# A transformer layer with routed experts: where the posts' weights are rounded, and the order of the work behind the attention

## The chip, the cores and the metric

The kernel runs on one core of a Trainium2 chip. The metric is the device time of one execution in microseconds. The core's engines run their own instruction streams and meet at semaphores: TensorE (PE in the profile; its weight loads are PEld), VectorE (DVE), ScalarE (ACT), GpSimd (POOL, "Pool" in the code) and SyncE (SP), which issues the DMA transfers.

## The reference

`x` is (4, 2048, 256) in float32: four sequences, 16 heads of 16 channels, 8 experts.

```python
# first: x = x + attn(layernorm(x)); attn adds its own input once more
qkv = einsum('bld,ed->ble', x, w_qkv) + b_qkv            # q, k, v: 16 heads of 16
attn = softmax(einsum('blhc,bmhc->bhlm', q, k) / 16)
heads = einsum('bhlm,bmhc->blhc', attn, v).reshape(b, l, d)
return einsum('bld,ed->ble', heads, w_o) + b_o + x
# then: x = x + ffn(layernorm(x)), with xf the 8192 tokens
scores = softmax(xf @ w_gate.T)                          # over the 8 experts
s = (scores + expert_bias).reshape(N, 4, 2)              # 4 groups of 2 experts
# keep the 2 groups with the largest sums, in them the 2 best experts: topk_idx
weights = take_along_axis(scores, topk_idx, 1)
counts = bincount(topk_idx.reshape(-1), length=8)
flat_idx = topk_idx.reshape(-1)                          # 16384 numbers of experts, 0 to 7
routed_in = xf[flat_idx] * weights.reshape(-1, 1)        # rows 0 to 7 of xf
h = silu(grouped_mm(routed_in, w1, counts)) * grouped_mm(routed_in, w3, counts)
routed_out = grouped_mm(h, w2, counts)
shared = silu(xf @ sw1.T) * (xf @ sw3.T) @ sw2.T
return shared.at[flat_idx].add(routed_out)               # into rows 0 to 7
```

Two things follow for the kernel. The routed experts' inputs are eight token rows only, scaled by a weight, so their products with `w1` and `w3` are small tables; and all 16,384 routed results are added into the first eight rows of the output, so they can be summed per expert and row, but not before the last token has been routed (`counts` sets which expert handles which row).

## The kernel before, in words

**Numbers.** Where float32 accuracy is wanted, an operand is held as two float32r tiles: a rounded high part and a low part, the difference. `mm3` multiplies high by high, high by low and low by high. `split` makes the two parts of a weight: ScalarE copies (the profile shows CAST), and the engine that it is given, or VectorE, subtracts.

**Units.** The 8192 tokens are 16 chunks of 512. The attention is 64 units of one sequence, four heads and one chunk. A unit has 64 `mx` matmuls (scores for the maxima, which VectorE reduces into `ms`; `finish_mx` transposes them into `mt` and sends them by DMA into row 63 of the unit's queries `qst`), 64 `st` matmuls (scores again, transposed, with the maximum taken off by that row), each with an exponential on ScalarE into `et`, and 128 `av` matmuls (values times `et`; the profile counts 8192 in all). A unit's result is copied out by ScalarE as `ao`. Keys come from DRAM into `kst`, 2 MB at a time. PSUM has one bank for `av` and seven for everything else (`mtile`).

**Posts.** A chunk whose four head groups are done gets its post: `post_first` loads the sums `s1` and heads `aT`, takes reciprocals on VectorE, sends them through DRAM to spread them over partitions (`rd`, `rb`) and has GpSimd scale `aT`; `post_a` multiplies by `w_o`, adds the residual `R`, normalises and calls `to_channels`, which transposes the result `x2` into `x2T` and its two parts; `route` makes logits (`lgT`, `lg`), softmax (`sc`, `sm`), ranks (`gt`, `eq`, `rk`) and one-hot picks `oh` with weights `wgt`; `shared` is the shared expert: `pa` and `pb` from `s_1` and `s_3`, a gate from tanh on ScalarE and GpSimd, then `pd` from `s_2`. A post's weights `w_o`, `s_1`, `s_3`, `s_2` are loaded and split by `setup`, a job that `enter` starts in unit 2. Its staging tile `wt` has two buffers.

**What sets the order.** All these jobs are generators in queues (`side`, `sums`, `norms`, `firsts`, `queue`, `posts`). Each yields what its next step needs: `need("m2", 705, tiles)` is a piece of TensorE work, "d" a VectorE piece, "a" and "p" a light piece of ScalarE or GpSimd, which is issued when by the planner's own clocks its tiles are ready; `gate` holds a job until a condition is true. The planner (`Plan`) books a cost for every instruction as it is written, and `Ahead.search` (random exchanges from a fixed seed) orders the next commands: M (`mx`), S (`st`), A (`av`), O (`ao`), P and D (pieces of the jobs). The search starts from the planner's state, so a change in one job's steps changes the order that it finds from there on. Within this loop the order on TensorE, VectorE, GpSimd and ScalarE is as written (`tc.manual_schedule`); behind it, before the change, a scheduler may reorder.

All instructions are issued through the planner's wrapper, so every line of the profile is L56. The names of tiles tell the work.

**The end.** The last chunk's post cannot overlap any attention. `last_heads` and `post_a` finish its heads; `to_channels` takes its fast path; then `finish` runs two generators in turn: `front` (the routing of the last chunk, then `moe`) and `behind` (`post_b`, its shared expert).

`moe` sums the experts. VectorE and TensorE count the picks (`m_cs`, `m_pc`, `m_tot`, `m_cum`). The 128 rows per partition are handled in 16 groups of 8: `ranges` (every fourth group) compares row numbers with the counts (`m_ge`, `m_oe`: the expert that handles a row); `pick` forms a one-hot `ob` on VectorE and a weighted `ow` on GpSimd, and transposes `ob` on TensorE into `mo`, which VectorE copies into `oT`; `hidden` looks the tables up with matmuls `mu` and makes the gate `mth`, half on ScalarE, half by a product on VectorE and a sigmoid on ScalarE; `gather` adds `ow` times `mth` into the bank `pg`. Then a short closing part (`m_ph`, `m_pr`, `m_po`) multiplies by `w2` and writes eight rows. Before the change the loop has three stages:

```python
for g in range(NG + 2):
    ...
    if g < NG:
        pick(g)
    if 1 <= g <= NG:
        hidden(g - 1)
    if g >= 2:
        gather(g - 2)
```

Of the kernel before, what the change touches and what calls it, by code (L numbers as in the profile page):

```python
# [20 lines left out]
P = 128  # L21
# [385 lines left out]
def body(tc, B, L, cols, x, wqkv, bqk, wst, bst, bv, wo, bo, wg, w1, w2, w3, sw1, sw2, sw3, ebias, cst, pad, out):  # L407
# [21 lines left out]
    def need(kind, ns=0, *tiles, more=0, act=940):  # L429


        return kind, ns, tiles, more, act

    def gate(open_):

        return "g", open_, (), 0, 0
# [43 lines left out]
    def split(name, tmp, out=None, eng=None):  # L480

        h, l = out or [cp.tile([P, 2, tmp.shape[2]], F32R, tag=f"{name}{q}", name=f"{name}{q}") for q in "hl"]
        S.copy(h, tmp)
        (eng or V).tensor_tensor(l, tmp, h.bitcast(F32), ALU.subtract)
        return h, l

# [73 lines left out]
    def to_channels(src, name, keep=None, fast=False, out=None):  # L560

        h, l = out or hl(f"t_{name}")
        if not fast:
            for c in range(2):
                f = keep[:, c, :] if keep is not None else sb.tile([P, QC], F32, tag="qkf", name=f"f_{name}{c}", bufs=2)
                pt = stile(f"pt_{name}{c}")
                for i in range(TQ):
                    T.transpose(pt[:, i * P:(i + 1) * P], src[:, i, c * P:(c + 1) * P], ident)
                S.copy(f, pt)
                G.tensor_copy(h[:, c, :], f)  # L570
                G.tensor_tensor(l[:, c, :], f, h[:, c, :].bitcast(F32), ALU.subtract)
                if c == 0:
                    yield need("s1", 436, act=470)
            return h, l
        for c in range(2):
            pt = mtile(f"pt_{name}{c}")
            for i in range(TQ):
                T.transpose(pt[:, i * P:(i + 1) * P], src[:, i, c * P:(c + 1) * P], ident)
            S.copy(keep[:, c, :], pt)
            S.copy(h[:, c, :], pt)  # L580
            V.tensor_tensor(l[:, c, :], pt, h[:, c, :].bitcast(F32), ALU.subtract)
            yield
        return h, l

    mark = {}
# [244 lines left out]
    def moe():  # L830
# [9 lines left out]
        V.tensor_copy(tot, pc[0:E, 0:P])  # L840
        cum = mtile("m_cum")
        T.matmul(cum[:, 0:E + 1], tot, K["below"][0:E, :], start=True, stop=True)
        ge = sb.tile([P, NR, E + 1], BF16, tag="vst", name="m_ge", bufs=2)
        oe = sb.tile([P, NR, E], BF16, tag="hq", name="m_oe", bufs=2)
        gb = sb.tile([P, E, 32], F32, tag="qkf", name="m_gb", bufs=2)
# [2 lines left out]
        pg = ps_av.tile([P, QC], F32, tag="av", name="pg")  # L848
        GR = 8
        NG = NR // GR  # L850
        ows, oTs, ths = {}, {}, {}

        def ranges(r0, r1):
            n = r1 - r0
            V.tensor_tensor(ge[:, r0:r1], K["rows"][:, r0:r1].unsqueeze(2).broadcast_to([P, n, E + 1]),
                            cum[:, 0:E + 1].unsqueeze(1).broadcast_to([P, n, E + 1]), ALU.is_ge)
            V.tensor_tensor(oe[:, r0:r1], ge[:, r0:r1, 0:E], ge[:, r0:r1, 1:E + 1], ALU.subtract)

        def pick(g):
            sl = slice(g * GR, (g + 1) * GR)  # L860
            ob = sb.tile([P, GR, E, 8], BF16, tag="x", name=f"ob_{g}", bufs=2)
            ow = ows[g] = sb.tile([P, GR, E, 8], F32, tag="lo", name=f"ow_{g}", bufs=3)
            ee = oe[:, sl, :].unsqueeze(3).broadcast_to([P, GR, E, 8])
            V.tensor_tensor(ob, ee, of[:, sl, :].unsqueeze(2).broadcast_to([P, GR, E, 8]), ALU.mult)
            G.tensor_tensor(ow, ee, oj[:, sl, :].unsqueeze(2).broadcast_to([P, GR, E, 8]), ALU.mult)
            pt = mtile(f"mo_{g}")
            obf = ob.rearrange("p r e j -> p (r e j)")
            for q in range(GR // 2):
                T.matmul(pt[:, q * P:(q + 1) * P], obf[:, q * P:(q + 1) * P], identb, start=True, stop=True)
            oT = oTs[g] = sb.tile([P, GR // 2, P], F32R, tag="hi", name=f"oT_{g}", bufs=3)  # L870
            V.tensor_copy(r2(oT), pt)
# [20 lines left out]
                         start=g == 0 and q < 2, stop=g == NG - 1 and q >= GR - 2, tile_position=(0, k))  # L892

        STEP = 4
        for g in range(NG + 2):
            if g % STEP == 0 and g < NG:
                ranges(g * GR, min(NR, (g + STEP) * GR))
            if g < NG:
                pick(g)
            if 1 <= g <= NG:  # L900
                hidden(g - 1)
            if g >= 2:
                gather(g - 2)
            if g == NG // 2:
                for h in range(2):
                    w_2.append(f4(f"w2_{h}").rearrange("p t (e n) -> p (t e) n", n=D))
                    Q.dma_start(w_2[h], w2[4 * h:4 * h + 4].rearrange("e p n -> p e n"))
            yield
# [19 lines left out]
    def post_first(b, c, nh=H):  # L928

        n = f"{b}_{c}"  # L930
        w = H * QC // P
        yield gate(lambda: f4_free(2) and sum({"a": 1, "x": -1}.get(x[0], 0) for x in f4s) == 0)
        aT, rb = f4(f"aT_{n}"), f4(f"rb_{n}")
        s1 = sb.tile([P, w], F32, tag="s1", name=f"s1_{n}", bufs=1)[0:nh * QC // w, :]
        tok = slice(c * QC, (c + 1) * QC)
        Q.dma_start(s1, ad[b][0:nh, 16, tok].rearrange("h (a n) -> h a n", n=w))
        parts = [(t, min(P, 16 * nh - P * t)) for t in range(2) if 16 * nh > P * t]
        for t, np_ in parts:
            Q.dma_start(aT[0:np_, t, :], ad[b][8 * t:8 * t + np_ // 16, 0:16, tok])
        yield need("d", 480, s1)  # L940
        V.reciprocal(s1, s1)
        rd = dr.tile([H * QC], F32, tag="rd", name=f"rd_{n}", bufs=2)
        Q.dma_start(rd[0:nh * QC].rearrange("(p n) -> p n", n=w), s1)
        for t, np_ in parts:
            Q.dma_start(rb[0:np_, t, :], rd[8 * t * QC:(8 * t + np_ // 16) * QC].rearrange("(h q) -> h q", q=QC)
                              .unsqueeze(1).broadcast_to([np_ // 16, 16, QC]))
        yield need("p", 2600, rb, aT)
        for t, np_ in parts:
            G.tensor_tensor(aT[0:np_, t, :], aT[0:np_, t, :], rb[0:np_, t, :], ALU.mult)
        f4_dead.add(f"rb_{n}")  # L950
        scaled[b, c] = aT, parts
# [37 lines left out]
        x2hl = yield from to_channels(x2, f"x2{n}", keep=x2T, fast=fast, out=space)  # L989
        return ch, n, x1, x2T, x2hl  # L990

    last = {}

    def post_last():

# [67 lines left out]
            V.tensor_tensor(xv, pd, xv, ALU.add)  # L1063
        write(ch, x1)

    def post_b(ch, n, x1, x2T, x2hl, rt, eng=G, hhl=None):

        hT = f4(f"hT_{n}")
        hhl = hhl or hl(f"hT_{n}")
        for m in range(2):  # L1070
            pa = mtile(f"pa_{n}_{m}")
            mm3(pa, W["s_1"], x2hl, slice(m * P, (m + 1) * P), slice(0, QC))
            th = sb.tile([P, QC], F32, tag="sth", name=f"th_{n}_{m}", bufs=2)
            S.activation(th, pa, AF.Tanh, scale=0.5)
            if eng is G:
                yield
            if eng is None:
                S.copy(hT[:, m, :], pa)
                G.tensor_tensor(th, th, K["ones"][:, 0:1].broadcast_to([P, QC]), ALU.add)
                G.tensor_tensor(th, th, hT[:, m, :], ALU.mult)  # L1080
            else:
                V.scalar_tensor_tensor(th, th, 1.0, pa, ALU.add, ALU.mult)
            yield
            next(rt, None)
            yield
            pb = mtile(f"pb_{n}_{m}")
            mm3(pb, W["s_3"], x2hl, slice(m * P, (m + 1) * P), slice(0, QC))
            if eng is None:
                S.mul(hT[:, m, :], pb, 0.5)
                G.tensor_tensor(hT[:, m, :], hT[:, m, :], th, ALU.mult)  # L1090
            else:
                V.scalar_tensor_tensor(hT[:, m, :], pb, 0.5, th, ALU.mult, ALU.mult)
            S.copy(hhl[0][:, m, :], hT[:, m, :])
            (eng or G).tensor_tensor(hhl[1][:, m, :], hT[:, m, :], hhl[0][:, m, :].bitcast(F32), ALU.subtract)
            yield
            next(rt, None)
            yield
        yield
        for half in range(2):
# [24 lines left out]
    def finish():  # L1124

        def front():
            p = last["q"] = yield from post_a(B - 1, NPER - 1, last["ahl"], (spare(0), spare(1)))
            yield from route(p[0], p[3])
            yield from moe()

        def behind():
            while "q" not in last:
                yield
            yield from post_b(*last["q"], iter(()), None)

        live = [front(), behind()]
        while live:
            for g in list(live):
                try:
                    next(g)  # L1140
                except StopIteration:
                    live.remove(g)


    queue, posts, side, norms, sums, firsts = (deque() for _ in range(6))
# [272 lines left out]
    def setup():  # L1418
# [4 lines left out]
        Q.dma_start(e_b, ebias.partition_broadcast(P))  # L1423
        for n, src in (("w_o", wo), ("s_1", sw1), ("s_3", sw3), ("s_2", sw2)):
            t = load_w(src, "sth", 2)
            yield need("a", 530, t)
            W[n] = split(n, t, eng=G)
        with tc.issue_after(mark["D"]):
            fill_rows(kd[0], 0, 0, 4)
# [348 lines left out]
```

## Time and profile before

| | before |
|---|---|
| median of 3 runs | 3067.62 us (3067.20 to 3068.33) |
| the profiled execution's own time | 3064.53 us |
| its span in the profile | 3062.7 us |
| mean granted TensorE clock | 0.986 |
| busy: PE, DVE, ACT, POOL | 2982.9, 2823.3, 2420.8, 649.9 us |
| instructions | 52745 |

Busy time by stretch, from the trace (us; the clock is the share of full speed that TensorE was granted):

| stretch of the span | length | PE | DVE | ACT | POOL | clock |
|---|---|---|---|---|---|---|
| 0 to 100: first chunks | 100.00 | 80.45 | 75.69 | 52.45 | 50.35 | 0.91 |
| 100 to 206 | 106.00 | 101.50 | 93.94 | 82.35 | 29.05 | 0.97 |
| 206 to 229: `setup` is in here | 23.00 | 12.84 | 10.23 | 9.24 | 7.85 | 0.70 |
| 229 to 2971.1: to the last `av` | 2742.10 | 2718.70 | 2585.46 | 2238.00 | 533.60 | 1.00 |
| 2971.1 to 3012.55: last chunk's post, to the first `mu` | 41.45 | 24.91 | 25.04 | 11.18 | 15.12 | 0.73 |
| 3012.55 to 3056.63: experts' sums | 44.08 | 42.37 | 31.59 | 27.58 | 13.95 | 0.94 |
| 3056.63 to the end | 6.07 | 2.10 | 1.35 | 0.00 | 0.00 | 0.93 |

How to read the profile: times in it come from one execution and are counted from the start of its span. A line of a timeline has the start, the length, the engine, the source line, the operation, output and input tiles with their shapes, and in brackets the idle time ahead of it with what ended it. A line of waits has the engine and work that waited, what it waited for, the total, the number of times and the longest. In the chain that ended last, a line has the start, the length and what was done. An engine that is busy for the whole of a stretch is not held up there; where none is, a wait or a chain sets the time.

### The profile page before, as it was taken

Reading aid. Unit: us, or ns where it says so; the run is one execution under the profiler, and the core shown is the slowest. Engines: PE = TensorE matmul, PEld = TensorE weight load, DVE = VectorE, ACT = ScalarE, POOL = GpSimd, SP = SyncE. Lnnn points to the kernel's source line nnn. Section 1 sums busy time; section 2 is a strip of 40 time slices with the busy share of each in tenths; the row PEclk is TensorE's granted clock in tenths of the full one; section 3 lists DMA queues with packets and bytes.
Section 4 is the critical chain, followed back from the end, with each engine's and each line's share of the span. In section 5 each row is a group of like instructions: output and inputs, shape, how many; then the busy total and the mean of one; then the engine's idle time right before and its main releaser. Section 6 shows DMA issues by size and latency. Waiting matters only on the chain.

```text
span 3062.7 us, 52745 instructions
## 1 busy us (share of the span) xinstructions
PE 2982.9 (97%) x19427; PEld 1359.8 (44%) x19427; DVE 2823.3 (92%) x5129; ACT 2420.8 (79%) x4745; POOL 649.9 (21%) x662
## 2 busy tenths in 40 slices
PE   7989999999999999999999999999999999999988
PEld 5434444444444444444444444444444444444436
DVE  7879999999999999999999999999999999999926
ACT  5578888888878878788888778888778788887774
POOL 5233223133213112110221220000222200023313
PEclk9899999999999999999999999999999999999998
DMA  5555645343121312221121200201121101011200
GB/s 157 184 156 151 167 114 162 94 140 112 51 94 40 115 32 88 64 79 69 44 86 39 72 25 20 90 22 69 45 75 49 69 25 58 31 54 40 77 26 15
DMA packets 144797, 237.32 MB, mean 77 GB/s; under 512 B 17115, under 2 KB 73563, under 8 KB 140379
## 3 DMA queue, kind: packets, MB, share of 16 engines
q1 hardware_dynamic: 144539, 233.96, 24.3%
q8 instruction: 153, 2.51, 0.3%
q14 instruction: 105, 0.86, 0.1%
HBM read 138.38 MB, written 111.80 MB: 82 GB/s over the span
## 4 chain that ended last, share of the span: by engine, by line
PE 80%; DVE 15%; DMA 1%; issue 1%; ACT 1%; POOL 1%; SPq 0%; POOLq 0%; ACTq 0%; DVEq 0%
PE av L56 29%; PE mx L56 20%; PE st L56 19%; DVE ms L56 11%; PE pp L56 3%; PE pd L56 2%; PE pv L56 1%; PE po L56 1%; PE pt_x L56 1%; PE pa L56 1%; PE pb L56 1%; PE mu L56 1%; ACT et L56 1%; PE pg L56 1%; DVE eq L56 1%
## 5 line engine op out<-in xcount | busy, mean ns | idle before, releaser
L56 DVE TENSOR_REDUCE ms<-mx 128x1 f32<-128x512 f32 x4096 | 2521.6, 682 | 135.0 <-PE mx L56 100.5
L56 ACT ACTIVATE et<-st 128x512 f32<-128x512 f32 x4096 | 2139.9, 611 | 440.4 <-PE st L56 288.2
L56 PE MATMUL mx<-kst,qst 63*128 63x512 f32 x3984 | 1222.7, 442 | 27.9 <-ACT et L56 10.6
L56 PE MATMUL st<-qst,kst 64*128 64x512 f32 x4032 | 1221.9, 440 | 7.3 <-DMA qst<-mt 3.4
L56 PE MATMUL av<-et,vst 128*32 128x512 f32 x8192 | 1098.4, 607 | 0.8 <-ACT ao L56 0.6
L56 PEld LDWEIGHTS mx<-kst,qst 63*128 63x128 f32 x3984 | 577.7, 186 | 605.8 <-DVE ms L56 289.8
L56 PEld LDWEIGHTS st<-qst,kst 64*128 64x128 f32 x4032 | 580.8, 186 | 556.1 <-DVE ms L56 278.9
L56 PEld LDWEIGHTS av<-et,vst 128*32 128x32 f32 x8192 | 164.0, 108 | 328.4 <-issue 307.7
L56 POOL TENSOR_TENSOR aT<-aT,rb 128x512 f32<-128x512 f32 (+1 forms) x32 | 40.9, 1285 | 571.3 <-DMA rb<-rd 570.9
L56 POOL CAST hi<-qkf 128x512 fp32r<-128x512 f32 x56 | 34.2, 610 | 328.3 <-ACT qkf L56 314.3
L56 POOL TENSOR_TENSOR lo<-qkf,hi 128x512 fp32r<-128x512 f32 x64 | 82.1, 1283 | 22.9 <-ACT hi L56 13.2
L56 ACT ACTIVATE qkf<-pp,b_qk 128x512 f32<-128x512 f32 x64 | 44.0, 687 | 53.8 <-PE pp L56 53.6
L56 POOL TENSOR_TENSOR th<-th,cs 128x512 f32<-128x512 f32 x32 | 33.5, 1046 | 222.8 <-ACT th L56 222.8
L56 POOL TENSOR_TENSOR rs_b<-rs_b,nhalf 128x4 f32<-128x4 f32 x16 | 16.3, 1017 | 279.7 <-DVE rs_b L56 279.7
L56 POOL TENSOR_TENSOR hT<-hT,th 128x512 f32<-128x512 f32 x32 | 41.0, 1281 | 123.7 <-ACT hT L56 47.4
L56 POOL TENSOR_TENSOR x<-x,xl 128x256 f32<-128x256 f32 x64 | 46.4, 755 | 16.8 <-ACT xl L56 16.8
L56 POOL TENSOR_TENSOR x<-x,b_o 128x256 f32<-128x256 f32 x64 | 45.5, 740 | 0.0
L56 ACT ACTIVATE xl<-x,rs_a 128x256 f32<-128x256 f32 x64 | 33.4, 594 | 11.1 <-DVE rs_a L56 11.0
L56 ACT COPY ao<-av 128x512 f32<-128x512 f32 x63 | 37.9, 601 | 3.0 <-PE av L56 2.0
L56 POOL TENSOR_TENSOR th<-th,sg 128x512 f32<-128x512 f32 x30 | 38.9, 1296 | 2.4
L56 ACT ACTIVATE th<-pa 128x512 f32<-128x512 f32 x32 | 19.2, 599 | 24.5 <-PE pa L56 24.2
L56 ACT ACTIVATE x<-x,rs_b 128x256 f32<-128x256 f32 x64 | 33.2, 597 | 6.6 <-DVE rs_b L56 6.6
(406 smaller groups left out, 2177.3 us busy)
## 6 DMA issues: line engine op xcount, KB each, us to landing
kst<-kd SPq DMA_DIRECT2D x16, 2048.0 KB
qst<-qd SPq DMA_DIRECT2D x63, 512.0 KB
qd<-hi SPq DMA_DIRECT2D x64, 256.0 KB
kd<-hi SPq DMA_DIRECT2D x64, 256.0 KB
ad<-ao SPq DMA_DIRECT2D x63, 256.0 KB
vst<-vd SPq DMA_DIRECT2D x19, 664.0 KB
vd<-vt SPq DMA_DIRECT2D x32, 332.0 KB
x<-x SPq DMA_DIRECT2D x16, 512.0 KB
```

Source lines behind the costliest of these rows:

```text
L56: r = f(*a, **k)
```

## The change

`setup`: the high parts of the posts' four weights are copied by GpSimd instead of ScalarE, and each weight's step waits until the planner's TensorE clock has advanced 12 us since its load was issued (`later`), and then for GpSimd. The reciprocals in `post_first` get the same gate. The fast path of `to_channels` transposes both halves first, copies both into `x2T`, then both high parts; the low parts are put off. `moe` reads the counts from an SBUF copy `cm`, and its loop has four stages: `pick` forms the one-hots, `turn` transposes them one step later, `hidden` runs two and `gather` three steps later, with `gather` ahead of the others. `post_b` runs its four products first, with tanh, copy and halving on ScalarE, and spreads its ten GpSimd steps beside the sums' loop; `pd` comes after these. All of `finish` is now in the order as written on PE, DVE, GpSimd and ScalarE.

```diff
@@ -431,6 +431,11 @@
 
         return kind, ns, tiles, more, act
 
+    def later(ns=12000):
+
+        t = plan.clock["PE"] + ns
+        return gate(lambda: plan.clock["PE"] > t)
+
     def gate(open_):
 
         return "g", open_, (), 0, 0
@@ -480,7 +485,7 @@
     def split(name, tmp, out=None, eng=None):
 
         h, l = out or [cp.tile([P, 2, tmp.shape[2]], F32R, tag=f"{name}{q}", name=f"{name}{q}") for q in "hl"]
-        S.copy(h, tmp)
+        (S.copy if eng is None else eng.tensor_copy)(h, tmp)
         (eng or V).tensor_tensor(l, tmp, h.bitcast(F32), ALU.subtract)
         return h, l
 
@@ -572,14 +577,21 @@
                 if c == 0:
                     yield need("s1", 436, act=470)
             return h, l
+        pts = []
         for c in range(2):
-            pt = mtile(f"pt_{name}{c}")
+            pts.append(mtile(f"pt_{name}{c}"))
             for i in range(TQ):
-                T.transpose(pt[:, i * P:(i + 1) * P], src[:, i, c * P:(c + 1) * P], ident)
-            S.copy(keep[:, c, :], pt)
-            S.copy(h[:, c, :], pt)
-            V.tensor_tensor(l[:, c, :], pt, h[:, c, :].bitcast(F32), ALU.subtract)
-            yield
+                T.transpose(pts[c][:, i * P:(i + 1) * P], src[:, i, c * P:(c + 1) * P], ident)
+            S.copy(keep[:, c, :], pts[c])
+        for c in range(2):
+            S.copy(h[:, c, :], pts[c])
+
+        def low():
+            for c in range(2):
+                V.tensor_tensor(l[:, c, :], pts[c], h[:, c, :].bitcast(F32), ALU.subtract)
+
+        last["low"] = low
+        yield
         return h, l
 
     mark = {}
@@ -840,6 +852,8 @@
         V.tensor_copy(tot, pc[0:E, 0:P])
         cum = mtile("m_cum")
         T.matmul(cum[:, 0:E + 1], tot, K["below"][0:E, :], start=True, stop=True)
+        cm = sb.tile([P, E + 1], F32, tag="m_cm", name="m_cm", bufs=1)
+        V.tensor_copy(cm, cum[:, 0:E + 1])
         ge = sb.tile([P, NR, E + 1], BF16, tag="vst", name="m_ge", bufs=2)
         oe = sb.tile([P, NR, E], BF16, tag="hq", name="m_oe", bufs=2)
         gb = sb.tile([P, E, 32], F32, tag="qkf", name="m_gb", bufs=2)
@@ -848,23 +862,25 @@
         pg = ps_av.tile([P, QC], F32, tag="av", name="pg")
         GR = 8
         NG = NR // GR
-        ows, oTs, ths = {}, {}, {}
+        obs, ows, oTs, ths = {}, {}, {}, {}
 
         def ranges(r0, r1):
             n = r1 - r0
             V.tensor_tensor(ge[:, r0:r1], K["rows"][:, r0:r1].unsqueeze(2).broadcast_to([P, n, E + 1]),
-                            cum[:, 0:E + 1].unsqueeze(1).broadcast_to([P, n, E + 1]), ALU.is_ge)
+                            cm.unsqueeze(1).broadcast_to([P, n, E + 1]), ALU.is_ge)
             V.tensor_tensor(oe[:, r0:r1], ge[:, r0:r1, 0:E], ge[:, r0:r1, 1:E + 1], ALU.subtract)
 
         def pick(g):
             sl = slice(g * GR, (g + 1) * GR)
-            ob = sb.tile([P, GR, E, 8], BF16, tag="x", name=f"ob_{g}", bufs=2)
-            ow = ows[g] = sb.tile([P, GR, E, 8], F32, tag="lo", name=f"ow_{g}", bufs=3)
+            ob = obs[g] = sb.tile([P, GR, E, 8], BF16, tag="x", name=f"ob_{g}", bufs=2)
+            ow = ows[g] = sb.tile([P, GR, E, 8], F32, tag="et", name=f"ow_{g}", bufs=6)
             ee = oe[:, sl, :].unsqueeze(3).broadcast_to([P, GR, E, 8])
             V.tensor_tensor(ob, ee, of[:, sl, :].unsqueeze(2).broadcast_to([P, GR, E, 8]), ALU.mult)
             G.tensor_tensor(ow, ee, oj[:, sl, :].unsqueeze(2).broadcast_to([P, GR, E, 8]), ALU.mult)
+
+        def turn(g):
             pt = mtile(f"mo_{g}")
-            obf = ob.rearrange("p r e j -> p (r e j)")
+            obf = obs.pop(g).rearrange("p r e j -> p (r e j)")
             for q in range(GR // 2):
                 T.matmul(pt[:, q * P:(q + 1) * P], obf[:, q * P:(q + 1) * P], identb, start=True, stop=True)
             oT = oTs[g] = sb.tile([P, GR // 2, P], F32R, tag="hi", name=f"oT_{g}", bufs=3)
@@ -892,15 +908,18 @@
                          start=g == 0 and q < 2, stop=g == NG - 1 and q >= GR - 2, tile_position=(0, k))
 
         STEP = 4
-        for g in range(NG + 2):
+        for g in range(NG + 3):
+            last["at"] = g
             if g % STEP == 0 and g < NG:
                 ranges(g * GR, min(NR, (g + STEP) * GR))
+            if g >= 3:
+                gather(g - 3)
             if g < NG:
                 pick(g)
+            if 2 <= g < NG + 2:
+                hidden(g - 2)
             if 1 <= g <= NG:
-                hidden(g - 1)
-            if g >= 2:
-                gather(g - 2)
+                turn(g - 1)
             if g == NG // 2:
                 for h in range(2):
                     w_2.append(f4(f"w2_{h}").rearrange("p t (e n) -> p (t e) n", n=D))
@@ -937,6 +956,7 @@
         parts = [(t, min(P, 16 * nh - P * t)) for t in range(2) if 16 * nh > P * t]
         for t, np_ in parts:
             Q.dma_start(aT[0:np_, t, :], ad[b][8 * t:8 * t + np_ // 16, 0:16, tok])
+        yield later()
         yield need("d", 480, s1)
         V.reciprocal(s1, s1)
         rd = dr.tile([H * QC], F32, tag="rd", name=f"rd_{n}", bufs=2)
@@ -989,7 +1009,7 @@
         x2hl = yield from to_channels(x2, f"x2{n}", keep=x2T, fast=fast, out=space)
         return ch, n, x1, x2T, x2hl
 
-    last = {}
+    last = {"at": -1}
 
     def post_last():
 
@@ -1063,37 +1083,34 @@
             V.tensor_tensor(xv, pd, xv, ALU.add)
         write(ch, x1)
 
-    def post_b(ch, n, x1, x2T, x2hl, rt, eng=G, hhl=None):
-
-        hT = f4(f"hT_{n}")
-        hhl = hhl or hl(f"hT_{n}")
+    def post_b(ch, n, x1, x2T, x2hl):
+
+
+        hT, hhl = f4(f"hT_{n}"), hl(f"hT_{n}")
+        g2 = sb.tile([P, 2, QC], F32, tag="et", name=f"g2_{n}", bufs=6)
+        ths = [sb.tile([P, QC], F32, tag="sth", name=f"th_{n}_{m}", bufs=2) for m in range(2)]
         for m in range(2):
             pa = mtile(f"pa_{n}_{m}")
             mm3(pa, W["s_1"], x2hl, slice(m * P, (m + 1) * P), slice(0, QC))
-            th = sb.tile([P, QC], F32, tag="sth", name=f"th_{n}_{m}", bufs=2)
-            S.activation(th, pa, AF.Tanh, scale=0.5)
-            if eng is G:
-                yield
-            if eng is None:
-                S.copy(hT[:, m, :], pa)
-                G.tensor_tensor(th, th, K["ones"][:, 0:1].broadcast_to([P, QC]), ALU.add)
-                G.tensor_tensor(th, th, hT[:, m, :], ALU.mult)
-            else:
-                V.scalar_tensor_tensor(th, th, 1.0, pa, ALU.add, ALU.mult)
-            yield
-            next(rt, None)
+            S.activation(ths[m], pa, AF.Tanh, scale=0.5)
+            S.copy(hT[:, m, :], pa)
             yield
             pb = mtile(f"pb_{n}_{m}")
             mm3(pb, W["s_3"], x2hl, slice(m * P, (m + 1) * P), slice(0, QC))
-            if eng is None:
-                S.mul(hT[:, m, :], pb, 0.5)
-                G.tensor_tensor(hT[:, m, :], hT[:, m, :], th, ALU.mult)
-            else:
-                V.scalar_tensor_tensor(hT[:, m, :], pb, 0.5, th, ALU.mult, ALU.mult)
-            S.copy(hhl[0][:, m, :], hT[:, m, :])
-            (eng or G).tensor_tensor(hhl[1][:, m, :], hT[:, m, :], hhl[0][:, m, :].bitcast(F32), ALU.subtract)
+            S.mul(g2[:, m, :], pb, 0.5)
             yield
-            next(rt, None)
+        while last["at"] < 0:
+            yield
+        for m in range(2):
+            G.tensor_tensor(ths[m], ths[m], K["ones"][:, 0:1].broadcast_to([P, QC]), ALU.add)
+            yield
+            G.tensor_tensor(ths[m], ths[m], hT[:, m, :], ALU.mult)
+            yield
+            G.tensor_tensor(g2[:, m, :], g2[:, m, :], ths[m], ALU.mult)
+            yield
+            G.tensor_copy(hhl[0][:, m, :], g2[:, m, :])
+            yield
+            G.tensor_tensor(hhl[1][:, m, :], g2[:, m, :], hhl[0][:, m, :].bitcast(F32), ALU.subtract)
             yield
         yield
         for half in range(2):
@@ -1131,15 +1148,20 @@
         def behind():
             while "q" not in last:
                 yield
-            yield from post_b(*last["q"], iter(()), None)
+            for _ in range(3):
+                yield
+            last["low"]()
+            yield
+            yield from post_b(*last["q"])
 
         live = [front(), behind()]
-        while live:
-            for g in list(live):
-                try:
-                    next(g)
-                except StopIteration:
-                    live.remove(g)
+        with tc.manual_schedule(engines={ENG.Pool, ENG.DVE, ENG.PE, ENG.Activation}):
+            while live:
+                for g in list(live):
+                    try:
+                        next(g)
+                    except StopIteration:
+                        live.remove(g)
 
 
     queue, posts, side, norms, sums, firsts = (deque() for _ in range(6))
@@ -1423,7 +1445,8 @@
         Q.dma_start(e_b, ebias.partition_broadcast(P))
         for n, src in (("w_o", wo), ("s_1", sw1), ("s_3", sw3), ("s_2", sw2)):
             t = load_w(src, "sth", 2)
-            yield need("a", 530, t)
+            yield later()
+            yield need("p", 2600, t)
             W[n] = split(n, t, eng=G)
         with tc.issue_after(mark["D"]):
             fill_rows(kd[0], 0, 0, 4)
```

## The prediction

> **What bounds the kernel now.** I read the page's busy shares and its chain first, then the waits, then two stretches closely.
>
> ```profile
> span 3062.7 us, 52745 instructions
> PE 2982.9 (97%) x19427; PEld 1359.8 (44%) x19427; DVE 2823.3 (92%) x5129; ACT 2420.8 (79%) x4745; POOL 649.9 (21%) x662
> PE 80%; DVE 15%; DMA 1%; issue 1%; ACT 1%; POOL 1%; SPq 0%; POOLq 0%; ACTq 0%; DVEq 0%
> ```
>
> TensorE is busy 97% of the span and carries 80% of the chain: between 100 and 2971 us the attention loop is limited by TensorE, with VectorE's maxima close behind, and a stop of TensorE there is lost for good. The first stretch holds such a stop. The chain there (start, length, what):
>
> ```profile
> 206.12 6.66 DMA wt<-sw
> 214.78 6.25 DMA wt<-sw
> ```
>
> ScalarE's timeline (in brackets its idle time ahead of the instruction, and what ended it):
>
> ```profile
> 220.35 0.62 ACT L56 CAST s_3h<-wt 128x512 fp32r<-128x512 f32 x1 [6.94 <-DMA wt<-sw]
> ```
>
> The waits from 190 to 240 us (total, times, longest):
>
> ```profile
> PE mx L56 <- ACT et L56: 10.2, 2, 9.1
> ```
>
> And the stretch behind the stop (length; busy time of TensorE, weight loads, VectorE, ScalarE, GpSimd; granted clock; share and rate of the DMA engines):
>
> ```profile
> 222.20:229.00 6.80, 6.78 (x27) 2.18 (x29) 2.58 (x4) 3.09 (x6) 4.16 (x5) 0.52 0.28 84
> ```
>
> ScalarE's queue reaches the rounding copies of the posts' weights before the weights have landed. The exponentials stand behind these copies, TensorE needs a bank that an exponential has to free, and stops for 9.1 us (and once for 1.1). Then it runs at a granted clock of 0.52 for 6.8 us.
>
> The second stretch is the end. The attention's last matmul ends at 2971.1; 91.6 us follow: the last chunk's post and routing, then the experts' sums. From VectorE's timeline, the routing's first pieces:
>
> ```profile
> 2989.40 0.32 DVE L56 STREAM_TRANSPOSE lg<-lgT 128x128 f32<-128x128 f32 x1 [2.87 <-PE lgT L56]
> 2992.57 1.23 DVE L56 TENSOR_TENSOR sel<-sc,e_b 128x32 f32<-128x32 f32 x1
> ```
>
> From the chain, a steady stage of the sums and their last group:
>
> ```profile
> 3045.21 1.02 PE pg L56 x16
> 3046.24 0.33 PE mo L56 x4
> 3046.57 1.00 PE mu L56 x8
> ...
> 3053.29 1.16 PE mu L56 x8
> ...
> 3054.54 0.70 DVE mth L56
> ...
> 3055.27 0.64 ACT mth L56
> ...
> 3055.95 0.68 PE pg L56 x8
> ```
>
> The steady stage is bound by TensorE: 0.33 + 1.00 + 1.02 = 2.35 us per group of eight rows. The last four lines are a group with nothing to hide behind: `mu`, VectorE's product, ScalarE's sigmoid, the second half of `pg`.
>
> **Setup.** The four ScalarE copies go (617 ns each), and with them the waits for the weights. Gain: 9.1 + 1.1 us of stops, and 6.8 x (1 - 0.52) = 3.3 us of half clock: 13.5 us. A second reading agrees: units' output copies `ao` on ScalarE lie 45.3, 58.6 and 45.5 us apart, and the long one holds the stop: 13.2 us. Bounds: 9.1 (the long stop alone) to 14. What is added lies on GpSimd: four casts at 610 ns, beside the four subtractions at 1.27 us that it had already; it is busy 21%. In the built program's order its `s_3h` cast stands between the two halves of the next chunk's transposed tokens, so a late weight would now hold that chunk's projections. The loads took 3.2, 6.7 and 6.3 us from issue to use; 12 us covers them. Without that cover one late load costs up to the 6.9 us that ScalarE waited. On SyncE the loads of weights two to four move behind the 2 MB `kst` load and the next chunk's stores; that `kst` is first used over half a unit later, so 0.
>
> **The reciprocal 12 us later.** It is a gate of the planner, not an instruction. The 15 full reciprocals had 0.0 us of idle VectorE before them, so nothing is gained; behind it waits only GpSimd's scaling, which idles 571 us for its broadcast already. 0.
>
> **The loop's order.** It is searched anew from the first changed job on. The built program has the same matmuls, 2606 changes of kind against 2613, and as many post matmuls at the start of units 59, 60 and 63. Mean effect 0. Its spread: units 39 to 44 and 53 to 57 hold no projections or post matmuls in either program, yet took 40.8 and 39.4 us each before. If a redraw moves 60 units by half that difference, independently, the total moves by about 0.7 x 7.7 = 5.5 us either way. The last maximum now comes after the four `av` rows that covered part of its 3.41 us wait for the transfer: +0.5.
>
> **The end, up to the first `mu`.** (1) The logits' matmuls stood mixed with `pa` and `pb`; now they come first, and both `x2T` copies come ahead of both `kst` ones. `x2T` ends about 2985.0, the matmuls 0.6 to 0.9 later, so `lg` starts at 2985.9: -3.5. (2) From there to `sm` it took 2.5; now 0.75 and two low parts at 0.65: -0.45. (3) From `sm` at 2991.91 to the counts' end at 3004.31 it took 12.4 us. Six pieces of 1.2 to 1.4 us ran while GpSimd worked on the post's gates; their like elsewhere are 0.2 to 0.45. With the gates moved behind the start of the sums the pieces add up to 6.2: -6.2. (4) From the counts to the first `ob` it took 4.6, in which `m_cum` waited behind the `pd` matmuls that now come later, and VectorE added `x`. The new copy of `cum` (0.2) is in the 3.05 that remain, as is up to 1 us for `pa` and `pb` at half clock: -1.55. (5) From `ob` to `mu` 3.65; now 3.15 to 3.65, since GpSimd still works beside both `ob`: -0.25. Sum -11.95: `mu` starts at 3000.6 instead of 3012.55. Bounds -9 to -13.
>
> **The sums.** The new stages are `pg`(g-3), `mu`(g-2), `mo`(g-1), and the built program has exactly this on TensorE. So between a group's `mu` and its own `pg` lies only one `mo`, 0.33 us; before there lay a whole stage, 2.35. From the last four lines: `mu` starts at 0, VectorE's product at 1.25, the sigmoid at 1.98, the second half of `pg` at 2.66, and its eight rows at 64 ns take 0.51. Then comes the next `mu`: 3.17 us per stage, bound by that chain, TensorE at work for 2.35 of it, 74%. GpSimd needs 1.05 + at most 1.30 per stage, VectorE 0.69 + 0.61 + 0.68: both below 3.17, so the gates are free; at a stage of 2.35 GpSimd would just become the bound. The two halves of `pd` (1.4 us each) fill part of the gaps and add 0.55 each.
>
> At half clock (`mu` rows 214 instead of 120 ns) a stage is 1.96 + 0.72 + 0.68 + 1.05 = 4.4. With three such at the start: 3 x 4.4 + 13 x 3.17 + 1.1 + 0.2 = 55.7, against 3056.63 - 3012.55 = 44.1 before: +11.6. Bounds +6 (no half clock, the product 0.2 earlier) to +18 (half clock half of the time, VectorE waiting for GpSimd).
>
> That the clock stays up at 74% rests on two rows: from 3020 to 3026 TensorE was busy 4.36 of 6 us at 1.00; from 2993.6 to 2997.0 it was busy 1.36 of 3.4, and the next windows show 0.75 and 0.50. I go by these rows. The Trainium skill's page "TensorE: Matmul & The Clock Gate" (HAM oscillation) asks only that no gap exceed about 3.4 us, where the gaps ahead of this fall were 2.0 and 2.1; by the page no stage would be slow and the time an estimated 3050.6.
>
> GpSimd beside VectorE: two `ob` took 3.00 us together while GpSimd ran, 0.68 each when it did not. In a steady stage I count 0.68, because GpSimd's two pieces end by 2.4 and `ob` starts at 2.6. The skill's page "SBUF — State Buffer" (two separate sides) speaks against the change here: a VectorE instruction with two SBUF inputs and a GpSimd one lock each other out for their whole length. By that, with `ob` always on the wrong side of a 1.30 us gate, ten stages would be 3.28, an estimated 1.1 us more.
>
> **Sum.** -13.5 + 0.5 - 11.95 + 11.6 = -13.35 us on the profiled execution (3064.53: its span and 1.8 around it). The median of the runs is 3067.62, 3.1 above that, which is taken over: 3054.3. What a measurement of this kernel can tell from no change is about 0.2%, 6.1 us: faster is below 3061.5.
>
> **Rivals.**
> - *The sums gain as well* (0.06): `pg` does not wait and the stage stays 2.35. Then they take 37.6 + 5 = 43: 3041.5. Against it: the program's order, and the four lines.
> - *The clock falls in the gaps* (0.10): sixteen stages at 4.4 make 71.7, +27.6 instead of +11.6: 3070.3, no change; with half of them, 3060. For it: the fall at 2997; against: the row from 3020.
> - *The stop comes back elsewhere* (0.10): the DMA engines are at a share of 0.7 to 1.0 from 208 to 220, and what now runs there without a pause has loads and stores of its own. GpSimd once waited 7.1 us for a `qd` store. Half to all of the 13.5 returns: 3061 to 3068.
> - *Slower* (0.05): the redrawn order costs more than the stop. It decides from (13.35 + 6.1)/62 = 0.32 us per unit on, a quarter of the 1.4 between the two stretches above; at 0.5 per unit 3085.
> - *The redraw is lucky* (0.08): 0.15 us per unit, 9 us: 3045.
>
> **How the numbers follow.** The forecast has the rest, 0.61, with 3047 to 3061.5 for itself. Faster: 0.61, 0.06, 0.08, half of the clock's case and a little of the returning stop: 0.82. Same 0.13, slower 0.05. The range reaches from the lucky redraw to half-way into the returning stop: 3045 to 3064.
>
> **What would show it.** In the profile after: no wait of ScalarE for `wt`, no stop near 213 and a unit of about 45 us there (else the setup step is wrong); the attention's end some 13 us earlier; the first `mu` 29.5 us behind it instead of 41.4; the routing's pieces at 0.2 to 0.45; a stage of 3.17 at a clock of 1.00 with `pg` waiting for ScalarE's `mth`. If the attention's end lies over 6 us from there, the redraw was mis-sized; if the stage is 2.35, the chain was misread.

## The result: slower, and the profile after

The changed kernel took 3078.76 us (median of 5 runs, 3077.05 to 3086.90), the kernel before 3067.20 (5 runs, 3062.13 to 3068.33). The ratio is 1.0042, 95% interval 1.0031 to 1.0053: 12 us slower, where 13 us less was forecast. The profiled execution after took 3077.45 us, with a span of 3075.5.

The page after, beside its lines in the prediction (span, busy time, chain by engine):

```profile
span 3075.5 us, 52784 instructions
PE 2996.0 (97%) x19427; PEld 1360.8 (44%) x19427; DVE 2822.6 (92%) x5130; ACT 2416.9 (79%) x4739; POOL 656.3 (21%) x668
PE 76%; DVE 18%; issue 2%; DMA 2%; ACT 1%; POOL 1%; SPq 0%; POOLq 0%; DVEq 0%; ACTq 0%
```

The number of matmuls is the same and VectorE's busy time too, but VectorE carries 18% of the chain instead of 15%.

**The setup did what was forecast.** GpSimd's timeline after has the four rounding copies, with no idle time ahead of any of them:

```profile
215.01 0.62 POOL L56 CAST w_oh<-wt 128x512 fp32r<-128x512 f32 x1
...
226.22 0.62 POOL L56 CAST s_1h<-wt 128x512 fp32r<-128x512 f32 x1
...
238.48 0.62 POOL L56 CAST s_3h<-wt 128x512 fp32r<-128x512 f32 x1
...
248.03 0.62 POOL L56 CAST s_2h<-wt 128x512 fp32r<-128x512 f32 x1
```

No wait of TensorE is left between 195 and 260 us. The `ao` copies of units 1 and 2 lie 46.1 us apart instead of 58.6.

**The loop lost it again, and more.** From unit 3's `ao` to the end of the last `av` it took 2667.5 us before (303.63 to 2971.09) and 2688.7 after (291.11 to 2979.76): +21.2. The windows of this stretch (length; busy PE, PEld, DVE, ACT, POOL; clock; DMA share; rate), before:

```profile
303.60:2971.10 2667.50, 2644.10 (x17352) 1167.63 (x17352) 2517.23 (x4574) 2174.75 (x4250) 508.27 (x501) 1.00 0.22 70
```

and after:

```profile
291.10:2979.80 2688.70, 2655.89 (x17340) 1165.10 (x17336) 2521.28 (x4573) 2172.85 (x4249) 508.18 (x500) 0.99 0.22 70
```

The work is the same: 17352 and 17340 matmuls in the trace. TensorE's longest waits in it (total, times, longest), before:

```profile
PE mx L56 <- DVE ms L56: 7.2, 8, 1.7
PE st L56 <- DMA qst<-mt: 3.4, 1, 3.4
PE st L56 <- DVE ms L56: 2.0, 3, 1.3
```

and after:

```profile
PE st L56 <- DVE ms L56: 9.8, 13, 3.1
PE st L56 <- DMA qst<-mt: 4.6, 1, 4.6
PE mx L56 <- DVE ms L56: 4.2, 8, 1.4
```

TensorE waits 14.0 us for VectorE's maxima instead of 9.2. These are only the stops that are long enough to be listed as waits. The start times of the matmuls say more: between two score matmuls (`mx` or `st`) that follow each other, 191 intervals above 0.4 us made 101 us before, 239 made 134 us after. All such intervals together, short ones included, took 937.9 us before and 961.9 after: 24.0 more, so they hold the loop's whole loss. And the clock record has half speed for 17.1 us of the stretch before, 34.1 after. That is worth up to 8.5 us; part of it lies in the same intervals, so the two are not added.

**The end.** The first `mu` came 32.1 us behind the last `av` instead of 41.5; the sums took 57.6 us instead of 44.1. From the chain after, one stage of the sums:

```profile
3024.84 1.15 PE mu L56 x8
...
3026.09 0.70 DVE mth L56
...
3026.82 0.64 ACT mth L56
...
3027.50 0.66 PE pg L56 x8
3028.16 1.16 PE mu L56 x8
```

It is the forecast's chain, step for step: from `mu` to VectorE's product 1.25, to the sigmoid 1.98, to the second half of `pg` 2.66. Only the last piece took 0.66 instead of 0.51, and so the stage is 3.32 instead of 3.17.

In all, from before to after: setup -12.5, loop +21.2, up to the first `mu` -9.4, sums +13.6: +12.9, and the spans differ by 12.8.

### The profile page after: what moved, and what is told of

Read it like the earlier page. It is cut to its first block, busy times and chain, and to the rows that moved or that the text cites. A ratio compares the mean times of both kernels' runs of the same rounds, so it can differ in the third digit from the quotient of the medians.

```text
span 3075.5 us, 52784 instructions
## 1 busy us (share of the span) xinstructions
PE 2996.0 (97%) x19427; PEld 1360.8 (44%) x19427; DVE 2822.6 (92%) x5130; ACT 2416.9 (79%) x4739; POOL 656.3 (21%) x668
## 4 chain that ended last, share of the span: by engine, by line
PE 76%; DVE 18%; issue 2%; DMA 2%; ACT 1%; POOL 1%; SPq 0%; POOLq 0%; DVEq 0%; ACTq 0%
PE av L56 27%; PE st L56 19%; PE mx L56 18%; DVE ms L56 13%; PE pp L56 2%; PE pd L56 2%; PE po L56 2%; PE pv L56 1%; PE pt_x L56 1%; PE pb L56 1%; PE pa L56 1%; DMA qd<-hi 1%; DVE eq L56 1%; DVE gt L56 1%; PE mu L56 1%
## 5 line engine op out<-in xcount | busy, mean ns | idle before, releaser
L56 PE MATMUL mx<-kst,qst 63*128 63x512 f32 x3984 | 1212.1, 441 | 17.3 <-DVE ms L56 8.0
L56 ACT ACTIVATE qkf<-pp,b_qk 128x512 f32<-128x512 f32 x64 | 44.1, 690 | 53.6 <-PE pp L56 53.3
```

Source lines behind the costliest of these rows:

```text
L56: r = f(*a, **k)
```

## The experiments

The questions were two: is the loop's loss in the change's steps or in the order being drawn anew, and what would setup and end be worth without it? Each median is given with that of before in the runs beside it.

**1. The new end alone.** The changed kernel with these lines taken back, so that the loop is before's:

```diff
-        (S.copy if eng is None else eng.tensor_copy)(h, tmp)
+        S.copy(h, tmp)
...
-        yield later()
         yield need("d", 480, s1)
...
-            yield later()
-            yield need("p", 2600, t)
+            yield need("a", 530, t)
```

> The new end (finish, moe, post_b, to_channels) on the setup, the reciprocals and therefore the loop's order of before. In the traces of before and after the first `mu` came 9.4 us sooner behind the last `av` (41.45 to 32.09) and the sums took 13.6 us longer (44.08 to 57.66). Theory 'the end itself costs': 3067.2 + 4.2 = 3071.4, the attention's end at about 2971 as before, a stage of the sums of 3.3 us. Rival 'the end only suffered from what came before it (its state at the attention's end)': 3067.2 - 0.4 = 3066.8, as the forecast had it.

3070.77 against 3068.99, ratio 1.0007 (0.9998 to 1.0016). The trace: stretch of the loop 2667.2, first `mu` after 30.8, sums 57.6; against before's trace 10.7 less and 13.5 more. VectorE and ScalarE run the same instructions in the same order as before up to the last `av`. The end itself gains nothing; it costs 2.8 us by the traces and 1.8 by the medians, whose interval includes no change.

**2. The end with its stages in another order.** As run 1, with `ow` taken out of `pick` into a function `weigh`:

```diff
-            if g >= 3:
-                gather(g - 3)
             if g < NG:
                 pick(g)
-            if 2 <= g < NG + 2:
-                hidden(g - 2)
             if 1 <= g <= NG:
                 turn(g - 1)
+            if 2 <= g < NG + 2:
+                hidden(g - 2)
+            if g >= 3:
+                gather(g - 3)
+            if g < NG:
+                weigh(g)
```

> As the run with the new end alone, but the four stages in another order within the loop: ob(g), mo(g-1), mu(g-2), pg(g-3), then ow(g); between a group's mu and its pg there is a whole stage again. Theory 'a stage is the chain mu, VectorE, ScalarE, pg': the stage falls from 3.3 to 2.35, the sums from 57.7 to about 47, the time to 3071.4 - 10.6 = 3060.8. Rival 'GpSimd beside VectorE sets the stage': it stays at 2.8 to 3.3 while the gates run, 10 of 16 stages: 3065 to 3071.

3060.19 against 3068.99, ratio 0.9972 (0.9961 to 0.9984), 10.6 less than run 1; the sums took 45.5. Its chain:

```profile
3026.88 0.99 PE mu L56 x8
3027.87 1.02 PE pg L56 x16
3028.90 0.33 PE mo L56 x4
3029.22 1.00 PE mu L56 x8
```

With a stage between a group's `mu` and its `pg` TensorE runs without a pause here, 2.34 us per stage, with the same gates on GpSimd. So the chain made the stage, and the better front is kept. The run's rival, GpSimd beside VectorE, shows in one stage: it took 4.5 us, with `m_ge` and `m_oe` on the chain, which took 1.35 and 1.27 us beside GpSimd's gates and 0.46 and 0.33 ahead of the loop.

**3 and 4. Before with another seed.** One number in `Ahead` is changed, no step of the kernel:

```diff
-        self.random = Random(1).random
+        self.random = Random(2).random
```

> The kernel before, with nothing changed but the seed of the search's random numbers (2 instead of 1). Theory 'a draw': the loop's order of before was a good draw, and another costs 5 to 25 us without any step of the change: 3072 to 3092, the attention's end at 2976 to 2996, and the loss again in the intervals between score matmuls. Rival 'the 12 us gate ahead of the reciprocals (or GpSimd's casts) makes every order worse': another seed alone moves the time by under 4 us: 3063 to 3071.

> The kernel before with seed 3, a second draw. Theory 'a draw': 3072 to 3092. Rival 'the gate or the casts': 3063 to 3071.

Seed 2: 3095.91 against 3068.99, ratio 1.0083 (1.0066 to 1.0099). Seed 3: 3082.36, ratio 1.0048 (1.0033 to 1.0063). The random numbers alone cost 27 and 13 us, as much as the whole change did or more. In the stretch of the loop seed 2 took 2699.5 us, 32.1 more than before, and TensorE's waits for VectorE there made 15.5 us:

```profile
PE st L56 <- DVE ms L56: 7.9, 9, 2.1
PE mx L56 <- DVE ms L56: 7.6, 11, 2.2
```

**5. The setup alone**, searched anew, with before's end and without the gate ahead of the reciprocals.

```diff
-            yield need("a", 530, t)
+            yield later()
+            yield need("p", 2600, t)
```

(and the copy in `split` on the engine given).

> The kernel before with the change's setup alone (copies on GpSimd, 12 us gate ahead of them, searched anew), without the gate ahead of the reciprocals and with before's end. Theory 'a draw': the stop goes (-13), and a new order costs 5 to 30: 3061 to 3086, most likely 3074. Rival 'the gate ahead of the reciprocals made the loss of the change': 3056, with no loss behind unit 3.

3071.29 against 3069.51, ratio 1.0009 (0.9998 to 1.0020). The stop is gone (unit 2 took 46.1 us), and the loop's stretch is 15.8 us longer. The gate ahead of the reciprocals is not in this kernel, so it cannot be the cause of this loss.

**6 and 7. The changed kernel with seeds 2 and 3.**

> The changed kernel with seed 2. Theory 'a draw': with the same steps as the changed kernel (3078.8) the time moves by 5 us or more either way: 3065 to 3095. Rival 'systematic': within 3 us of the changed kernel, 3076 to 3082.

> The changed kernel with seed 3. Theory 'a draw': from the four redrawn orders so far, which cost 14 to 32 us between unit 3 and the last av over before's order: 3070 to 3092. Rival 'the changed kernel's order is an unlucky one, and another gives the forecast back': under 3062.

Seed 2: 3089.84 against 3069.51, ratio 1.0073 (1.0052 to 1.0095). Seed 3: 3073.79 against 3069.20, ratio 1.0017 (1.0007 to 1.0026). The same steps, 16 us apart.

**8. The gate ahead of the reciprocals alone**, on before.

```diff
+        yield later()
         yield need("d", 480, s1)
```

> The kernel before with the 12 us gate ahead of the reciprocals alone. The loop starts to differ only where the first reciprocal comes, in unit 13. Theory 'a draw': up to there as before, with the stop; after it 8 to 25 us more: 3077 to 3095. Rival 'the gate is free and the order does not matter': 3066 to 3072.

3089.95 against 3069.20, ratio 1.0068 (1.0053 to 1.0083). The units before the first reciprocal are as before; then the order differs, and the stretch is 23.2 us longer.

**9. The copies on GpSimd, the order kept.** The planner books the copies on ScalarE, so that it decides as before; there is no gate.

```diff
-        S.copy(h, tmp)
+        if eng is None:
+            S.copy(h, tmp)
+        else:
+            nc.gpsimd.tensor_copy(h, tmp)
+            plan.book_act("copy", h, [tmp], {})
```

> The kernel before with the four rounding copies of the posts' weights issued on GpSimd, while the planner books them on ScalarE as before: the loop keeps before's order to the last instruction, only these four copies change their engine, and there is no 12 us gate. Theory 'the stop goes, the redraw cost the rest': no wait of ScalarE for the weights, the unit with the stop at 45 to 47 us instead of 58.6, and nothing lost later: 3069.0 - 13 = 3056 (3054 to 3060, if GpSimd's queue, which now waits for each weight, holds some work up). Rival 'what lies behind the copies on GpSimd is late instead' (rs_a, hi, lo came at 223.5 in before and would now be wanted some 13 us sooner): the stop comes back half or whole: 3062 to 3069.

3068.91 against 3069.51, ratio 0.9998 (0.9988 to 1.0008): nothing. Its chain:

```profile
213.99 12.12 DMA wt<-sw
...
226.16 0.62 POOL s_3h L486
...
228.74 1.26 POOL s_2l L56
...
230.00 0.99 POOL rs_a L56
231.01 0.55 DVE rs_a L56
```

and TensorE's wait from 190 to 260 us:

```profile
PE mx L56 <- DVE ms L56: 10.2, 1, 10.2
```

The stop has only changed its path. GpSimd now waits for the weights, behind them stands the next chunk's `rs_a`, VectorE waits for it, and TensorE for VectorE. The engine is not what removes the stop; the rival was right here.

**10. The same with the end of run 2.**

> The same, with the end of the run in which pg lies a whole stage behind mu. If the two gains are independent: 3060.2 - 13 = 3047 (3045 to 3051), faster than both kernels. By the rival of the run with the same order alone: 3053 to 3060.

3055.95 against 3069.51, ratio 0.9956 (0.9943 to 0.9969). The stop is there as in run 9 (unit 2 took 56.1 us), the end as in run 2.

**11. Earlier loads, the order kept.** The copies stay on ScalarE and the four compute engines keep before's order entirely; the loads are issued in unit 1 instead of unit 2, into two `sth` and one `r` buffer, and booked where they were. The traces show VectorE, ScalarE and GpSimd with the same instructions in the same order up to the last `av`.

```diff
-            t = load_w(src, "sth", 2)
+            t = ready[n]
+            plan.book_sp("dma_start", t, [src.rearrange("(t p) n -> p t n", p=P)], {})
             yield need("a", 530, t)
...
+        if u == 1:
+            early()
```

> The kernel before with the order of its four compute engines kept to the last instruction and the copies on ScalarE as before; only the loads of the posts' four weights are issued a unit sooner, into other buffers, so that they have landed when the copies come. Theory 'time, not the engine, takes the stop away': no wait for wt, the unit with the stop 45 to 47 us instead of 58, and everything after it as in before: 13 us less, 3056 (3053 to 3059). Rival 'the DMA engines are the limit there, and what waits for them only changes': the stop stays in another place, 3062 to 3070.

3058.43 against 3069.20, ratio 0.9962 (0.9950 to 0.9973). Three of the four copies on ScalarE, none of which waits:

```profile
211.45 0.61 ACT L56 CAST s_1h<-wt 128x512 fp32r<-128x512 f32 x1
211.96 0.62 ACT L56 CAST s_3h<-wt 128x512 fp32r<-128x512 f32 x1
212.48 0.62 ACT L56 CAST s_2h<-wt 128x512 fp32r<-128x512 f32 x1
```

Unit 2 took 45.75 us instead of 58.57, 12.8 less, and the loop's stretch 2666.8: nothing was given back.

**12. Earlier loads with the end of run 2.**

> Early loads in before's order, and the end with pg a whole stage behind mu. If both gains hold and add: 3069 - 13 - 9 = 3047 (3044 to 3050), the fastest of all here. By the rival of the run with early loads alone: 3055 to 3060.

3043.50 against 3069.20, ratio 0.9916 (0.9901 to 0.9932): 25.7 us less than before, the fastest of all. It has the change's two ideas, time for the loads and the new end, with the order kept and the stages turned. The gains of runs 2 and 11 add up to 19.6; by the traces the part up to unit 3's `ao` gave 12.5, the end 9.5 and the loop's stretch 3.5, where the clock record has half speed for 6.8 us instead of 17.1; among the other executions in before's order it differs as much (10.2 to 23.9).

The loop's stretch in all fourteen traces (from unit 3's `ao` to the last `av`'s end; score intervals above 0.4 us, whose number is good to about 3, since some lie at 0.4 itself; time at half clock):

| order | kernel | length | intervals, us | half clock |
|---|---|---|---|---|
| before's | before | 2667.5 | 191, 101 | 17.1 |
| before's | runs 1, 2, 9, 10, 11, 12 | 2664.0 to 2669.0 | 187 to 192, 101 to 102 | 6.8 to 23.9 |
| another | after | 2688.7 | 239, 134 | 34.1 |
| another | 3: before, seed 2 | 2699.5 | 259, 143 | 44.4 |
| another | 4: before, seed 3 | 2681.5 | 234, 127 | 34.1 |
| another | 5: setup alone | 2683.3 | 229, 124 | 23.9 |
| another | 6: after, seed 2 | 2691.6 | 254, 138 | 27.3 |
| another | 7: after, seed 3 | 2678.9 | 216, 119 | 23.9 |
| another | 8: gate alone | 2690.6 | 214, 124 | 41.0 |

Seven executions in before's order lie within 5 us; seven other orders lie 11 to 32 us above before, 20 on average. With the gate ahead of the reciprocals (after, 6, 7, 8) they are 20 above on average, without it (3, 4, 5) 21.

## Why the prediction was wrong

**The step that failed** is "The loop's order": "Mean effect 0", with a spread of 5.5 us. Measured, the new order cost 21.2 us, and orders drawn anew cost 20 on average. Two things in the step were wrong. It took the order before as a typical draw, about which others scatter evenly; but all seven others were worse, by 11 us at least. And it took equal counts (matmuls, changes of kind) as a sign of equal time, where the time lies in the waits between score matmuls, which the counts don't show. In the seven traces the intervals between score matmuls hold 17 of the 20 us on average. The size of the spread came out near: the seven orders have a standard deviation of 7 us. As it was drawn from two stretches of one order, as if units were independent, that is partly luck. The mean was mis-sized, not the spread. Without the loop's 21.2 us the changed kernel would stand at 3057.6, inside the forecast's 3045 to 3064.

The rival "slower: the redrawn order costs more than the stop" had the place right: at 21.2 us over 60 units it is 0.35 us per unit, just past the point of 0.32 from which the text let it decide (19.45 over 62 is 0.31). With a mean of 20 for the redraw instead of 0 the forecast's own sum would have been +6.7, just past the 6.1 from which it calls a kernel slower.

**Setup: right in size, and in the condition.** Forecast -13.5, measured -12.5 in the changed kernel and -12.8 with the order kept (run 11). That the copies go to GpSimd is not what gains: run 9 shows the stop of 10.2 us in GpSimd's queue. The prediction had said that 12 us cover the loads and that without that cover a late load holds the next chunk's work; run 9 is this case, with a stop of 10.2 us where the text had put up to 6.9. The rival of a stop that comes back elsewhere did not occur in the changed kernel; it did in run 9.

**The reciprocal's gate: 0**, as far as the averages above can tell; its own effect cannot be told apart from the new order that it brings.

**The end up to the first `mu`: right in sign, 2.6 short.** Forecast -11.95, measured -9.36. By its steps: to `lg` -3.5 was forecast and -1.0 measured (17.3 us behind the last `av` instead of 18.3). The forecast step itself held: from the first transpose of `x2` to `lg` it took 4.2 us instead of 7.6, -3.4. But the transposes start 2.4 us later, since ScalarE's normalised `x`, which they read, comes 12.5 us behind the last `av` (2979.8) instead of 10.0 (2971.1), before and after:

```profile
2981.11 2.08 ACT L56 ACTIVATE x<-x,rs_b 128x256 f32<-128x256 f32 x4 [6.56 <-DVE rs_b L56]
2992.22 2.08 ACT L56 ACTIVATE x<-x,rs_b 128x256 f32<-128x256 f32 x4 [8.99 <-DVE rs_b L56]
```

The sum had put this piece, the part of `post_a` ahead of the transposes, at nothing. About half of it comes with the order as written: in run 1 the transposes start 1.2 us later too, with the `po` matmuls at full clock. In both, VectorE's statistics of `x` come only behind both additions of `R`; before the change they began between the two. The other half came, in the changed kernel's trace, with a clock at half speed from 3.7 to 7.1 us behind the last `av`, where the `po` matmuls run. In run 1 the whole step was -2.2. To `sm` 1.88 was measured for 2.05, the ranks and counts 6.13 for 6.2, from the counts to `ob` 3.88 for 3.05, from `ob` to `mu` 2.90 for 3.4.

**The sums: right, and a little small.** Forecast 55.7, measured 57.6 in the changed kernel and 57.6 to 57.7 in runs 1, 6 and 7. The stage was 3.32 instead of 3.17, since a half of `pg` that starts afresh takes 0.66 and not 8 x 64 ns; the last of the four lines from which the forecast read the chain had 0.68. The first three stages took 12.9 for the 13.2 forecast, by luck: the clock was at half speed only up to 3021.0, for two of them (5.3 and 4.3 us for the 4.4 forecast; a table load of 1.28 us on ScalarE is on the chain of the first), and the third took 3.3. After 3024.8 the clock stayed at 1.00, as the rows said. Once GpSimd was on the path, which had been put at 0: a late step of the shared expert's gates still read the buffer that `mth` takes (ScalarE's timeline after, idle time and what ended it in brackets):

```profile
3039.66 1.14 ACT L56 ACTIVATE mth<-mu,wgt 128x128 f32<-128x128 f32 x4 [2.28 <-POOL hT_3l L56]
```

This stage took 3.9 us, 0.6 more. So the end as a whole cost 4.2 us where -0.35 was forecast. The stage of 2.35 on which the rival "the sums gain as well" counted was there in run 2, with the stages turned, and not in the changed kernel. The rule of the Trainium skill's page "SBUF — State Buffer" (two separate sides) shows in the rows: `ob` took 1.61 us at 3030.6 and 1.25 at 3037.2 beside GpSimd's pieces, each time ending 0.55 us behind the end of such a piece, and 0.68 without them. In the time of these sums it does not show, since neither was on the chain; in run 2's stage of 4.5 us it does.

**Still open** is why before's order is so good. The seeds show that chance in the search is enough to lose 14 and 32 us in the loop, and the traces show where most of the time goes; what a good order has that the others lack no run tells.

## What to carry to other kernels

Where an edit makes a search draw its order anew, price the redraw first: change the seed alone, in two or three builds, and take their mean and spread as a term of the sum, since the order at hand need not be a typical one. To find what the edit itself is worth, keep the order, by letting the planner book what it booked before; here the order kept, with earlier loads and the stages turned, made a gain of 26 us out of a loss of 12. And in a pipeline of stages look at how far a result's first reader is behind it in the order as issued: four stages with the wrong neighbours were slower than three.

## What the runs showed of the hardware

In the midst of dense work the clock fell to half behind a single short stop. TensorE started matmuls at 1543.1 and 1545.0 and none between, 1.4 us of which it stood idle, and the changed kernel's clock record shows half speed for 3.4 us from 1546.5 on. The window around it:

```profile
1540.00:1550.00 10.00, 8.60 (x49) 3.36 (x47) 9.86 (x20) 7.04 (x14) 3.19 (x2) 0.83 0.01 2
```

Such a spell loses 1.7 us, which the stop can cost on top of itself. The stretch after holds seven spells of 3.4 us and a longer one behind the wait for `mt`. Four of the seven had a gap of 1.8 to 3.5 us between the starts of two matmuls in the 4 us ahead of them. A stop is not the only way there: ahead of the spells at 1491.8 and 1792.2 no two matmuls started over 0.65 us apart, and what halved the clock there is open. The Trainium skill's page "TensorE: Matmul & The Clock Gate" (HAM oscillation) puts the limit for a gap at about 3.4 us; here 1.9 us between starts, 1.4 of them idle, came ahead of such a fall, and the measurement decides.
